# W1 loaded in two transfers with 1 KB pieces, and x transposed from every second column

## The chip, the cores and the metric

The kernel runs on one core of one Trainium2 chip. A core has five engines that run beside each other: TensorE (PE, with its weight loads shown apart as PEld), VectorE (DVE), ScalarE (ACT), GpSimd (POOL) and SyncE (SP), which here only issues transfers (DMA). Data comes from the main memory into SBUF (128 partitions); TensorE writes into PSUM, from where DVE and ACT read. The metric is the time of one execution in microseconds of device time, lower is better.

## The reference

`x` has 128 batches of 128 rows and 512 columns in float32. Each batch has a language id `itok` between 0 and 8, which picks one of ten sets of weights. The bottleneck layer, residual and normalization are

```
w1 = W1[language_ids]                      # [512, 128] of each batch
w2 = W2[language_ids]                      # [128, 512] of each batch
h = jnp.einsum('bsh,bha->bsa', hidden_states, w1) + b1[language_ids][:, None, :]
h = jax.nn.relu(h)
adapted = jnp.einsum('bsa,bah->bsh', h, w2) + b2[language_ids][:, None, :]
x = hidden_states + adapted
mean = jnp.mean(x, axis=-1, keepdims=True)
var = jnp.mean(jnp.square(x - mean), axis=-1, keepdims=True)
normed = (x - mean) * jax.lax.rsqrt(var + LN_EPS)
return normed * gamma[language_ids][:, None, :] + beta[language_ids][:, None, :]
```

and the output is the input `x` plus that result. `W1` is [10, 512, 128]: language, input column h, bottleneck column a.

## The kernel before, in words

A batch is one tile: its 128 rows lie on the 128 partitions, its 512 columns in the free dimension. `x` is loaded in groups of four batches (`load_x`, line 67, 1 MB each, with four buffers), all weights of all ten languages are loaded once at the start and stay in SBUF, and each batch picks its language's slice by a register.

**The start.** SP issues its transfers in this order (lines 85 to 108): the ids, gamma, the first two batches of x (`load_part(0, 2)`, line 83), W1 in four transfers (line 97), the other two batches of the first group, W2 in two transfers of five languages each (line 102), and the groups x_1, x_2 and x_3. ACT issues beta, b2 and b1. W1's tile `w1` is [128 partitions, 10 languages, 4 chunks, 128]. Transfer k brings chunk k: partition p gets row 128k + p of each language's W1, so a piece that is contiguous on both sides is one row of 128 values, 512 B. x and W2 come in pieces of 2 KB.

While these flow, TensorE runs some idle matmuls (`spin`, line 418), transposes the first batches, and spreads the rows of beta, gamma and b2 over all partitions (`spread`, line 155), which DVE and ACT copy out (lines 158 and 160). Then follow the down projections of batches 0 to 3, then up(0), up(1), up(2).

**One batch.** `stage_w1` (line 186): ACT copies the language's [128, 4, 128] slice of `w1` into `w1s`. `transpose_x` (line 191): TensorE turns the four chunks of 128 columns of x, one transpose each, into the PSUM tile pxT; here the chunk of x is the operand that is loaded as weights (the LDWEIGHTS records of line 191), and the identity is streamed through. `copy_xT` (line 195): ACT copies pxT to SBUF as xT. `down` (line 214): for each chunk k, w1s chunk k as weights, xT chunk k streamed, all four accumulated; as fp32, each is two passes in the profile. `relu` (line 222) on ACT. `up` (line 231), two passes of 512 columns; for the first four batches and one in four after that, a small bf16 matmul (line 230) adds b2, otherwise POOL does it (`add_b2`, line 201). POOL also prepares x + beta (`add_beta`, line 208). DVE adds the residual (line 237), centers and scales by gamma (line 281) and finishes (line 290); ACT makes the sum of squares (line 249).

**The order.** It is written out by hand: `keep` ties each instruction behind the one before it on its engine, queues included. In the steady loop the order on TensorE is transposes of batch i, down of batch i - 1, up of batch i - 2. pxT has a single buffer, so the transposes of a batch wait until ACT has copied the batch before out; py has five buffers. The chunks only have to agree between `w1` and the transposes: chunk k of xT must hold the columns of x that chunk k of `w1` holds as rows.

Of the kernel before, what the change touches and what calls it, by code (L numbers as in the profile page):

```python
# [16 lines left out]
P = 128  # L17
# [6 lines left out]
def cond_resid_kernel(ctx: ExitStack, tc: tile.TileContext, x, itok, W1, b1, W2, b2, gamma, beta, out):  # L24
# [8 lines left out]
    nc = tc.nc  # L33
    B, S, H = x.shape
    L, _, A = W1.shape
    KC = H // P
# [6 lines left out]
    def keep(ins):  # L43

        engine = ins.ins.engine
        if engine in last:
            tc.add_manual_dep(ins.ins, last[engine], behind, reason="kept order")
        last[engine] = ins.ins.name
        return ins
# [20 lines left out]
    def xb(b):  # L70
        return xs[b // G][:, b % G, :]
# [5 lines left out]
    w1 = const.tile([P, L, KC, A], FP, name="w1")  # L77
# [14 lines left out]
    warm = const.tile([P, 1], FP, name="warm")  # L92
    nc.vector.memset(warm, 1.0)
    keep(nc.scalar.activation(warm, warm, AF.Sqrt))
    for k in range(KC):
        keep(
            nc.sync.dma_start(out=w1[:, :, k, :], in_=W1[:, k * P : (k + 1) * P, :].rearrange("l p a -> p l a"))
        )
    load_part(2, G)
    for l in range(0, L, 5):  # L100
        keep(
            nc.sync.dma_start(
                out=w2[:, l * H : (l + 5) * H].rearrange("p (l h) -> p l h", l=5),
                in_=W2[l : l + 5].rearrange("l a h -> a l h"),
# [5 lines left out]
    ident = const.tile([P, P], FP, name="ident")  # L110
# [52 lines left out]
    phs, pxs, sums = {}, {}, {}  # L163
# [24 lines left out]
    def transpose_x(b):  # L188
        pxs[b] = p_x.tile([P, KC, P], FP, tag="xT", name=f"pxT_{b}")
        for k in range(KC):  # L190
            keep(nc.tensor.transpose(pxs[b][:, k, :], xb(b)[:, k * P : (k + 1) * P], ident))  # L191

    def copy_xT(b):
        xT[b] = tp.tile([P, KC, P], FP, tag="xT", name=f"xT_{b}")
# [228 lines left out]

    spin(12, H)
    transpose_x(0)
    transpose_b1()
    copy_xT(0)
    for r in range(22):
        spread(r, nc.scalar if r % 3 == 2 else nc.vector)
        if r == 5:  # L430
            transpose_x(1)
            copy_xT(1)
        elif r > 5:
            spin(1, H // 2)
# [3 lines left out]
    for b in range(4):  # L438
        down(b)
        if b < 2:  # L440
            transpose_x(b + 2)
        relu(b)
        if b < 2:
            copy_xT(b + 2)
        for r in range(22 + 3 * b, min(25 + 3 * b, R)):
            spread(r, nc.scalar if r % 3 == 2 else nc.vector)
        stage_w1(b + 2)
# [3 lines left out]
    for i in range(3, B + U):  # L451
        if i < B and i % G == 0 and i // G + 3 < NG:
            load_x(i // G + 3)
        b = i - U - 1
# [20 lines left out]
        p = g - 1  # L475
# [79 lines left out]
```

## Time and profile before

| | |
|---|---|
| median of three runs | 321.16 us (320.8 to 321.39) |
| the profiled execution: its time, its span | 321.39 us, 318.8 us |
| granted TensorE clock in it | 0.987 |
| PE, PEld busy | 305.1 us (96%), 226.0 us (71%) |
| DVE, ACT, POOL busy | 300.7 (94%), 285.5 (90%), 280.6 us (88%) |
| moved by DMA | 72.88 MB, 40,986 packets |
| transposes, L191: MATMUL, LDWEIGHTS | 512 of 273 ns, 512 of 141 ns |

The profile shows one execution; times in it count from the span's start. In a line of the order of time come the start, the length, the engine, the line of the kernel, the operation and its tiles; brackets tell how long the engine was idle just before, and what ended that. Neighbouring instructions of one kind are merged (x4). The records of matmuls overlap, since one drains while the next streams, so the work of TensorE is read from start to start. In a table of stretches each row gives the stretch, then the busy time and number of instructions of each engine, the granted clock, the share of the DMA engines and what they moved in GB/s.

### The profile page before, as it was taken

Reading aid. Unit: us, or ns where it says so; the run is one execution under the profiler, and the core shown is the slowest. Engines: PE = TensorE matmul, PEld = TensorE weight load, DVE = VectorE, ACT = ScalarE, POOL = GpSimd, SP = SyncE. Lnnn points to the kernel's source line nnn. Section 1 sums busy time; section 2 is a strip of 40 time slices with the busy share of each in tenths; the row PEclk is TensorE's granted clock in tenths of the full one; section 3 lists DMA queues with packets and bytes.
Section 4 is the critical chain, followed back from the end, with each engine's and each line's share of the span. In section 5 each row is a group of like instructions: output and inputs, shape, how many; then the busy total and the mean of one; then the engine's idle time right before and its main releaser. Section 6 shows DMA issues by size and latency. Waiting matters only on the chain. (4 is left out here: it accounts for less than half of the span.)

```text
span 318.8 us, 7184 instructions
## 1 busy us (share of the span) xinstructions
PE 305.1 (96%) x1889; PEld 226.0 (71%) x1889; DVE 300.7 (94%) x1000; ACT 285.5 (90%) x721; POOL 280.6 (88%) x234
## 2 busy tenths in 40 slices
PE   8998999999999999999999999999999999999960
PEld 3475777777777777777777777777777777777730
DVE  5946999999999999999999999999999999999995
ACT  2686989999999999999999999999999999999972
POOL 1306999999999999999999999999999999999873
PEclk9999999999999999999999999999999999999995
DMA  7997577577766666678666676678766666633324
GB/s 204 317 386 288 198 262 254 214 264 263 221 231 212 223 246 232 228 264 263 247 215 213 217 244 231 223 265 264 245 210 215 224 241 228 226 135 133 129 112 156
DMA packets 40986, 72.88 MB, mean 229 GB/s; under 512 B 1737, under 2 KB 6868, under 8 KB 40946
## 3 DMA queue, kind: packets, MB, share of 16 engines
q1 hardware_dynamic: 40886, 72.38, 66.4%
q8 instruction: 15, 0.25, 0.3%
q14 instruction: 25, 0.20, 0.2%
q10 hardware_dynamic: 60, 0.05, 0.1%
HBM read 38.86 MB, written 33.55 MB: 227 GB/s over the span
## 5 line engine op out<-in xcount | busy, mean ns | idle before, releaser
L208 POOL TENSOR_TENSOR o<-x,beta_b 128x512 f32<-128x512 f32 x128 | 162.0, 1278 | 10.6 <-DVE beta_b L160 10.6
L201 POOL TENSOR_TENSOR r<-x,b_b 128x512 f32<-128x512 f32 x93 | 118.8, 1277 | 20.0 <-DMA x<-in_x_dram 12.1
L214 PE MATMUL ph<-xT,w1s 128*128 128x128 f32 x1024 | 135.7, 275 | 0.3 <-ACT w1s L186 0.2
L231 PE MATMUL py<-w,hT 128*128 x256 | 130.9, 593 | 0.2 <-DVE o L290 0.2
L214 PEld LDWEIGHTS ph<-xT,w1s 128*128 128x128 f32 x1024 | 124.6, 192 | 2.6 <-ACT hT L222 1.3
L191 PEld LDWEIGHTS pxT<-ident,x 128*128 128x128 f32 x512 | 63.9, 141 | 67.1 <-issue 43.4
L281 DVE SCALAR_TENSOR_TENSOR py<-py,nmean,gamma_b 128x512 f32<-128x512 f32 x126 | 94.7, 752 | 0.3 <-issue 0.3
L290 DVE SCALAR_TENSOR_TENSOR o<-py,rstd,o 128x512 f32<-128x512 f32 x122 | 90.4, 741 | 1.4 <-DVE nmean L242 0.5
L249 ACT ACTIVATE sq<-py,nmean 128x512 f32<-128x512 f32 x124 | 85.3, 688 | 4.5 <-DVE nmean L242 2.9
L195 ACT COPY xT<-pxT 128x512 f32<-128x512 f32 x128 | 73.8, 577 | 12.1 <-PE pxT L191 10.1
L186 ACT COPY w1s<-w 128x512 f32 x128 | 79.5, 622 | 0.2 <-DVE gamma_b L160 0.2
L191 PE MATMUL pxT<-ident,x 128*128 128x128 f32 x512 | 77.0, 273 | 0.9 <-ACT xT L195 0.7
L237 DVE SCALAR_TENSOR_TENSOR py<-py,r 128x512 f32<-128x512 f32 x93 | 64.7, 695 | 2.5 <-POOL r L201 0.6
L222 ACT ACTIVATE hT<-ph,b1T 128x128 f32<-128x128 f32 x128 | 47.6, 372 | 1.1 <-PE ph L214 1.0
L231 PEld LDWEIGHTS py<-w,hT 128*128 128x128 f32 x256 | 41.6, 192 | 2.9 <-issue 0.9
L237 DVE SCALAR_TENSOR_TENSOR py<-py,x 128x512 f32<-128x512 f32 x35 | 24.2, 692 | 3.7 <-PE py L231 3.7
L249 ACT ACTIVATION_READ_ACCUMULATOR sq<-py,nmean 128x1 f32 x124 | 25.2, 203 | 0.0
L255 ACT ACTIVATE sd<-ssq,eps 128x2 f32<-128x2 f32 x62 | 18.3, 296 | 2.1
L242 DVE TENSOR_SCALAR nmean<-sum 128x1 f32<-128x1 f32 x128 | 18.7, 146 | 0.2
L230 PE MATMUL py<-parts,pick 96*128 96x512 bf16 x35 | 13.3, 381 | 0.0
L237 DVE DVE_READ_ACCUMULATOR py<-py,r 128x1 f32 x93 | 13.1, 141 | 0.0
L270 DVE TENSOR_TENSOR stat<-stat,y 128x2 f32<-128x2 f32 x62 | 12.8, 206 | 0.0
(54 smaller groups left out, 117.7 us busy)
## 6 DMA issues: line engine op xcount, KB each, us to landing
x<-in_x_dram SPq DMA_DIRECT2D x31, 1024.0 KB, 6.1
out_dram<-o SPq DMA_DIRECT2D x61, 512.0 KB, 3.5
w<-in_L_cond_W_dram SPq DMA_DIRECT2D x4, 640.0 KB, 6.6
w<-in_L_cond_W_dram SPq DMA_DIRECT2D x2, 1280.0 KB, 11.5
out_dram<-o SPq DMA_DIRECT2D x6, 256.0 KB, 2.2
x<-in_x_dram SPq DMA_DIRECT2D x2, 512.0 KB, 3.9
rows<-in_L_cond_beta_dram ACTq DMA_DIRECT2D x1, 20.0 KB
rows<-in_L_cond_gamma_dram SPq DMA_DIRECT2D x1, 20.0 KB
```

Source lines behind the costliest of these rows:

```text
L186: keep(nc.scalar.copy(w1s[b].rearrange("p k a -> p (k a)"), src))
L191: keep(nc.tensor.transpose(pxs[b][:, k, :], xb(b)[:, k * P : (k + 1) * P], ident))
L195: keep(nc.scalar.copy(xT[b], pxs.pop(b)))
L201: keep(nc.gpsimd.tensor_tensor(rs[b], xb(b), b2_b[:, bass.ds(v * H, H)], ALU.add))
L208: keep(nc.gpsimd.tensor_tensor(os[g][:, j, :], xb(b), beta_b[:, bass.ds(v * H, H)], ALU.add))
L214: nc.tensor.matmul(phs[b], lhsT=w1s[b][:, k, :], rhs=xT[b][:, k, :], start=(k == 0), stop=(k == KC - 1))
L222: keep(nc.scalar.activation(hT[b], phs.pop(b), AF.Relu, bias=b1T[:, bass.ds(lid(b, ET.Activation), 1)]))
L231: keep(nc.tensor.matmul(ys[b], lhsT=hT[b], rhs=w2[:, bass.ds(v * H, H)], start=not m, stop=True))
L237: keep(nc.vector.scalar_tensor_tensor(ys[b], ys[b], 1.0, r, ALU.mult, ALU.add, accum_out=s))
L249: keep(nc.scalar.activation(sq, ys[b], AF.Square, bias=nmeans[b], accum_out=ssqs[g][:, j : j + 1]))
L281: nc.vector.scalar_tensor_tensor(ys[b], ys[b], nmeans.pop(b), gamma_b[:, bass.ds(v * H, H)], ALU.add, ALU.mult)
L290: nc.vector.scalar_tensor_tensor(o, ys.pop(b), rstds[g][:, j : j + 1], o, ALU.mult, ALU.add)
```

## The change

W1 comes in two transfers. Transfer m brings the 256 rows 256m to 256m + 255 of each language, and partition p gets the two neighbouring rows 256m + 2p and 256m + 2p + 1, as chunks 2m and 2m + 1 of `w1`. A piece contiguous on both sides is two rows, 1 KB. Chunk 2m + j of `w1` so holds the rows 256m + 2p + j, and the transposes read the same columns of x: for chunk 2m + j those from 256m + j on, every second one, 128 of them. Everything else is as it was.

```
-    for k in range(KC):
+
+    for m in range(KC // 2):
         keep(
-            nc.sync.dma_start(out=w1[:, :, k, :], in_=W1[:, k * P : (k + 1) * P, :].rearrange("l p a -> p l a"))
+            nc.sync.dma_start(
+                out=w1[:, :, 2 * m : 2 * m + 2, :].rearrange("p l j a -> p l (j a)"),
+                in_=W1[:, 2 * m * P : 2 * (m + 1) * P, :].rearrange("l (p j) a -> p l (j a)", j=2),
+            )
         )
     load_part(2, G)
...
     def transpose_x(b):
         pxs[b] = p_x.tile([P, KC, P], FP, tag="xT", name=f"pxT_{b}")
         for k in range(KC):
-            keep(nc.tensor.transpose(pxs[b][:, k, :], xb(b)[:, k * P : (k + 1) * P], ident))
+            cols = xb(b).rearrange("s (m p j) -> s m j p", m=KC // 2, j=2)[:, k // 2, k % 2, :]
+            keep(nc.tensor.transpose(pxs[b][:, k, :], cols, ident))
```

## Prediction

> **What bounds the kernel now.** I read the stretches of the span first, then the groups by line, then the order of time in one steady stretch and in the start. From 100 to 300 us TensorE has no free time, and its clock is granted in full.
>
> ```profile
> core 0: us, PE busy (x) PEld busy (x) DVE busy (x) ACT busy (x) POOL busy (x), PEclk, DMA share, GB/s
> 8.00:10.00 2.00, 2.00 (x14) 1.30 (x13) 2.00 (x5) 1.66 (x3) 0.00 (x0) 1.00 1.20 290
> ...
> 16.00:18.00 2.00, 1.77 (x14) 1.52 (x14) 0.62 (x2) 1.23 (x3) 0.00 (x0) 1.00 1.05 387
> ...
> 100.00:200.00 100.00, 100.00 (x635) 75.87 (x634) 99.03 (x335) 96.15 (x247) 97.03 (x79) 1.00 0.69 237
> ```
>
> A busy PE is not yet PE at its peak, so I check it by the starts of its matmuls (columns: start, length, engine, line; lengths overlap, starts don't).
>
> ```profile
> 152.30 0.60 PE L191 MATMUL pxT<-ident,x 128*128 128x128 f32 x4
> 152.74 1.06 PE L214 MATMUL ph<-xT,w1s 128*128 128x128 f32 x8
> 153.63 1.02 PE L231 MATMUL py<-w,hT 128*128 x2
> 154.49 0.60 PE L191 MATMUL pxT<-ident,x 128*128 128x128 f32 x4
> ```
>
> From start to start: 0.44 us for 4 transposes (110 ns each), 0.89 for 8 down matmuls (111 each), 0.86 for two passes of up (430 each), 2.19 in all. One batch in four adds the b2 matmul: transposes start at 149.89, 152.30, 154.49, 156.68 and 158.87, so four batches take 8.98 us, 2.245 each. The pitches leave no gap. DVE, dense too at 99%, starts L237 of two batches at 154.86 and 157.03, 2.17 us apart: it follows closely. So whatever lengthens or shortens TensorE's order by a nanosecond per batch is seen 128 times, and whatever only moves a transfer counts just where TensorE waits for it.
>
> **The weight loads of the transposes.** In the transposes x is the operand that LDWEIGHTS loads and ident the one that streams; so the new step of two falls on LDWEIGHTS.
>
> ```profile
> 152.31 0.36 PEld L191 LDWEIGHTS pxT<-ident,x 128*128 128x128 f32 x3 [0.29 <-issue]
> 152.63 0.97 PEld L214 LDWEIGHTS ph<-xT,w1s 128*128 128x128 f32 x8
> 153.52 0.30 PEld L231 LDWEIGHTS py<-w,hT 128*128 128x128 f32 x2
> 154.06 0.14 PEld L191 LDWEIGHTS pxT<-ident,x 128*128 128x128 f32 x1 [0.24 <-ACT w1s L186]
> ```
>
> A batch's first load (154.06 to 154.20) runs beside the second pass of up, and has 0.29 us to spare before the transposes start at 154.49. The other three sit one behind the other with a pitch of (0.36 - 0.14) / 2 = 110 ns, the same as that of the matmuls that they feed. They have no cover at all.
>
> **The change, part by part.**
>
> *W1's transfers.* Four DMA issues of 1,280 pieces of 512 B become two of 1,280 pieces of 1 KB; the bytes stay (4 x 640 KB = 2.62 MB). The rows above price the pieces: 290 GB/s while W1's 512 B pieces flow (8 to 10 us), 387 while 2 KB pieces flow (16 to 18). W1 at 290 takes 9.04 us. No row has 1 KB pieces; the bounds are these two rates, 9.04 and 6.77 us, so W1 saves between 0 and 2.3 us. Between them I take a fixed part and a part per byte: over 16 engines a 512 B piece takes 28.2 ns and a 2 KB piece 84.7, so 1 KB takes 28.2 + 56.5/3 = 47 ns, 349 GB/s, 7.5 us: **W1 and all that is queued behind it on SP's queue lands 1.5 us earlier**. Against this stands the Trainium skill, "DMA: Bandwidth & Descriptors", section Specifications: 512 B is given there as the smallest transfer that reaches line rate, by which W1 would save nothing and the forecast would be no change; the trace differs, 290 against 387 GB/s.
>
> *Who waits for them.* SP issues, in order, x_0's first half, W1, x_0's second half, W2, x_1 to x_3. stage_w1(0) starts on ACT at 15.72 behind the row copies, 0.24 us after ACT's last; W1's pieces have given way to those of 2 KB by 14 us (the stretch from 14 to 16 moves 388 GB/s), so it isn't what held it. The down, transpose and row matmuls run without a DMA wait to 26.2. The first wait for a transfer is x_1's:
>
> ```profile
> 25.34 1.02 PE L231 MATMUL py<-w,hT 128*128 x2
> 26.59 0.63 PE L191 MATMUL pxT<-ident,x 128*128 128x128 f32 x4 [0.22 <-DMA x<-in_x_dram]
> 27.89 0.66 PE L191 MATMUL pxT<-ident,x 128*128 128x128 f32 x4 [0.68 <-ACT xT L195]
> ...
> 26.61 1.26 POOL L201 TENSOR_TENSOR r<-x,b_b 128x512 f32<-128x512 f32 x1 [12.13 <-DMA x<-in_x_dram]
> ```
>
> Two passes of up from 25.34 leave TensorE free at 25.34 + 0.86 = 26.20; the transposes of batch 4 start at 26.59. x_1 costs 0.39 us, and both TensorE and POOL (26.61) start as it lands. Landing 0.39 us earlier is enough; a W1 at 303 GB/s (2.62 MB in 8.65 us) would do it. What is late next is TensorE itself: up(2) ahead of these transposes, then copy_xT(4) on ACT, which the wait at 27.89 shows, and which moves with them. From 28.4 on TensorE is full, so the 0.39 is kept to the end. **-0.39 us** (bounds 0 and -0.39). POOL starts its r_4 earlier too; that is worth nothing, since DVE reads r_4 at 33.25, over 5 us after it was ready. x_2 and x_3 land earlier than they did, and TensorE never waited for them. Two DMA issues fewer on SP cost and gain nothing: nobody waits for SP in the start but for the data.
>
> *The step of two.* 512 loads of 128 columns read every second element over 1 KB in place of 512 B. No row has such a read. The nearest are the contiguous loads, 110 ns apart, and pick's broadcast loads of one element (step zero, 98 ns mean, bf16), which show no price for a pattern. Nothing is skipped in instructions or bytes used, so no gain; the lower end is 0. The upper end: the load takes as long as two contiguous loads of the span it covers, +110 ns, uncovered for three of four: 0.33 us x 128 = +42 us. I take **0**, as the row for the same number of columns is the nearest. The Trainium skill, "SBUF — State Buffer", section Door 1, says that full speed needs at least two accesses in each 16-byte line. A step of two over fp32 has exactly two, so the page makes it free, at the very edge; a step of four would not be. No run here shows it.
>
> *PSUM, copies, down.* pxT, xT, w1s keep their shapes; the copies and down matmuls read the same amounts in the same order. 0.
>
> **The sum.** The profiled execution took 321.39 us, span 318.8 and 2.6 around it: 321.39 - 0.39 = 321.0. That execution is the slowest of three; their median is 321.16, and the same step from it gives **320.8 us**.
>
> **The rivals.**
>
> *A. The strided load is slower (the other side).* Place: the three uncovered loads of each batch. Price: each ns adds 3 x 128 = 0.384 us. One ns eats the gain; from 2.7 ns (1.03 / 0.384) the kernel is slower by over 0.2%. A doubled load gives 321.0 + 42 = 363 us; 8 ns give 324. For it: the two pitches are equal, TensorE has no slack, 512 loads. Against it: nothing in the rows shows a price of a pattern. A small price 0.08, a large one 0.18.
>
> *B. The pieces of 1 KB flow no faster (the change doesn't do what it says for the queue).* x_1 lands as before: 321.2. For it: the 290 GB/s could be set by something other than the piece. Against: 2 KB pieces from the same memory on the same queue ran at 387 right behind. 0.07.
>
> *C. More is gained than x_1's wait.* With x_1 early, TensorE and ACT meet in another rhythm between 26 and 28.4, where TensorE is idle 0.39 and then 0.86 us (27.03 to 27.89). If all went: 319.9. Against: the second pause is copy_xT(4), 0.59 us, with pxT in a single buffer, which the change leaves. 0.07.
>
> **How the numbers follow.** The forecast has 0.60, its own range 320.3 to 321.4 by the scatter of the three runs (320.8 to 321.39) around the shift. What a measurement of this kernel can tell from no change is about 0.2%, 0.64 us. Forecast and B lie within it; of the forecast I give 0.10 to a measured time over 0.64 us below, so faster is 0.07 + 0.10 = 0.17. Slower is A, 0.26, and a little scatter: 0.27. Same is the rest, 0.56. The range goes from 320.1 (part of C) to 324.2 (the small price of A) and leaves out the large price.
>
> **What would show it.** Right: the rate between 6 and 12 us at some 350 GB/s with half the packets; the transposes of batch 4 at 26.2 with no DMA wait; L191's LDWEIGHTS at a mean of 141 ns, a pitch of 110, and four batches in 8.98 us. Wrong: a longer mean or pitch of L191's LDWEIGHTS, matmuls of L191 apart by more than 110 ns, and PEld busier than 76% between 100 and 200 us, which would make it rival A; 290 GB/s in place of 350, rival B.

## The result, and the profile after

The changed kernel takes 323.88 us (median of 22 runs, 322.96 to 324.99) against 320.95 us before (22 runs, 320.03 to 322.48): ratio 1.0091, 95% interval 1.0080 to 1.0102. It is 0.9% slower. The forecast was 320.8 us, a little faster: the direction is the wrong one, and the time lies in the stated range only because the range took in the small price of rival A.

Between 100 and 300 us TensorE is as dense as it was. The group rows of the transposes, line 196 in the changed kernel (busy us, then mean ns of one), point to where the time came from: the weight loads have a mean of 202 ns in place of 141, their matmuls 281 in place of 273, and the down matmuls stay at 275.

```profile
L219 PE MATMUL ph<-xT,w1s 128*128 128x128 f32 x1024 | 135.5, 275 | 0.2
L196 PEld LDWEIGHTS pxT<-ident,x 128*128 128x128 f32 x512 | 80.7, 202 | 59.8 <-issue 36.8
L196 PE MATMUL pxT<-ident,x 128*128 128x128 f32 x512 | 81.1, 281 | 0.7 <-ACT xT L200 0.7
```

A mean of overlapping records isn't a price yet. The order of time gives it, one batch, matmuls and then weight loads (start, length, engine, line):

```profile
153.33 0.63 PE L196 MATMUL pxT<-ident,x 128*128 128x128 f32 x4
153.80 1.06 PE L219 MATMUL ph<-xT,w1s 128*128 128x128 f32 x8
154.69 1.02 PE L236 MATMUL py<-w,hT 128*128 x2
155.55 0.63 PE L196 MATMUL pxT<-ident,x 128*128 128x128 f32 x4
```

```profile
152.91 0.20 PEld L196 LDWEIGHTS pxT<-ident,x 128*128 128x128 f32 x1 [0.24 <-ACT w1s L190]
153.33 0.44 PEld L196 LDWEIGHTS pxT<-ident,x 128*128 128x128 f32 x3 [0.23 <-issue]
153.68 0.98 PEld L219 LDWEIGHTS ph<-xT,w1s 128*128 128x128 f32 x8
```

From the first transpose to the first down matmul it is 0.47 us, 0.44 before; the rest of the batch is unchanged (0.89 and 0.86). Read one by one, the starts of these matmuls are 109, 117, 120 and 120 ns apart where they were 109 four times: 8 + 11 + 11 = **30 ns a batch**. The first strided load, beside a pass of up, costs nothing; the other three do. Four batches take 9.10 us (transposes at 150.89 and 159.99) in place of 8.98. Over 128 batches 30 ns are 3.84 us.

The transfers did what they were to do. W1's pieces flow at some 350 GB/s (stretches, last column):

```profile
8.00:10.00 2.00, 2.00 (x14) 1.30 (x12) 2.00 (x4) 1.58 (x3) 0.00 (x0) 1.00 1.10 348
10.00:12.00 2.00, 2.00 (x13) 1.11 (x12) 2.00 (x4) 1.25 (x3) 0.00 (x0) 1.00 1.11 352
...
14.00:16.00 2.00, 1.71 (x10) 0.84 (x9) 2.00 (x4) 1.05 (x3) 0.77 (x1) 1.00 1.05 388
```

and the transposes of batch 4, and POOL's first r, no longer follow x_1:

```profile
25.64 1.02 PE L236 MATMUL py<-w,hT 128*128 x2
26.50 0.63 PE L196 MATMUL pxT<-ident,x 128*128 128x128 f32 x4
```

```profile
23.74 1.27 POOL L206 TENSOR_TENSOR r<-x,b_b 128x512 f32<-128x512 f32 x1 [8.97 <-DMA x<-in_x_dram]
```

Batch 4 starts without a wait, but at 26.50, only 0.09 us earlier than the 26.59 of before: up(2) ends 0.30 us later. The first row matmuls start at 7.42 us, 7.14 before, since in this execution the four transposes of batch 0 ran 213 ns apart until 6.9 us; before, the third interval was 110 ns.

From there to the last matmul (26.51 to 310.60, before 26.59 to 307.62) it is 3.06 us more. That is 124 batches of 30 ns, 3.7, less 0.6 us that a second effect gave back: before, TensorE paused for 0.3 us at 48.6 and again at 67 us, after it didn't.

That second effect starts at DVE. Before the change DVE sat idle for 0.63 us until 42.77, and for 0.55 until 61.02. After such a gap ACT has to wait for DVE's `nmean`, its copies are late, and TensorE waits for pxT to be copied out. The rows of the kernel before, of DVE, ACT, and PEld near 48 and 66 us:

```profile
42.77 0.70 DVE L237 SCALAR_TENSOR_TENSOR py<-py,r 128x512 f32<-128x512 f32 x1 [0.63 <-POOL r L201]
```

```profile
44.23 0.69 ACT L249 ACTIVATE sq<-py,nmean 128x512 f32<-128x512 f32 x1 [0.41 <-DVE nmean L242]
```

```profile
48.17 0.51 PEld L191 LDWEIGHTS pxT<-ident,x 128*128 128x128 f32 x4 [0.52 <-ACT xT L195]
...
66.42 0.53 PEld L191 LDWEIGHTS pxT<-ident,x 128*128 128x128 f32 x4 [0.50 <-ACT xT L195]
```

The bracket of the first row names POOL's r, but POOL had long been done: the r that DVE reads at 42.77 is r_8, which POOL wrote from 35.22 to 36.50.

```profile
35.22 1.28 POOL L201 TENSOR_TENSOR r<-x,b_b 128x512 f32<-128x512 f32 x1
```

What ended just before 42.77 is DVE's own load of the next four language ids into registers (`lid`, line 168 before, 172 after), from 41.41 to 42.61. Such instructions aren't counted as busy, so the time looks idle. The rows of that load, before and after (duration in ns, start in us):

```profile
L168 DVEq TENSOR_LOAD <-lang x1: 1201/1201/1201, 41.4 to 41.4; - x1
```

```profile
L172 DVEq TENSOR_LOAD <-lang x1: 626/626/626, 41.4 to 41.4; - x1
```

In all 14 profiles, each of the 18 gaps of DVE over 0.2 us between 38 and 303 us is as long as the load in front of it less 0.57 us; after the short load here the gap is 0.05. Why the load takes 1.20 us at one time and 0.63 at another isn't shown.

### The profile page after: what moved, and what is told of

Its sections match the earlier page's. It is cut to its first block, busy times and chain, and to the rows that moved or that the text cites. A ratio compares the mean times of both kernels' runs of the same rounds, so it can differ in the third digit from the quotient of the medians.

```text
span 322.2 us, 7180 instructions
## 1 busy us (share of the span) xinstructions
PE 308.5 (96%) x1889; PEld 236.8 (74%) x1889; DVE 304.7 (95%) x1000; ACT 284.1 (88%) x721; POOL 281.1 (87%) x234
## 5 line engine op out<-in xcount | busy, mean ns | idle before, releaser
L219 PEld LDWEIGHTS ph<-xT,w1s 128*128 128x128 f32 x1024 | 125.9, 193 | 1.9 <-ACT hT L227 0.8
L196 PEld LDWEIGHTS pxT<-ident,x 128*128 128x128 f32 x512 | 80.7, 202 | 59.8 <-issue 36.8
L196 PE MATMUL pxT<-ident,x 128*128 128x128 f32 x512 | 81.1, 281 | 0.7 <-ACT xT L200 0.7
```

The source lines that it names most:

```text
L196: keep(nc.tensor.transpose(pxs[b][:, k, :], cols, ident))
L219: nc.tensor.matmul(phs[b], lhsT=w1s[b][:, k, :], rhs=xT[b][:, k, :], start=(k == 0), stop=(k == KC - 1))
```

## The experiments

My theory after the result: the strided loads cost 30 ns a batch, where they have no cover; the transfers alone are a gain. The first rival: the transfers' new landing times upset the rhythm, and the loads are innocent. The second: every strided load costs alike, covered or not. Each kernel of an experiment was run 4 to 12 times, beside the kernel before.

The measured time is the span and what lies around it, which is not the same in all runs: mostly 1.8 us, in others up to 3.2. So the table gives the median span too, and I compare small differences by spans.

| kernel | us | ratio to before, 95% | median span (before) |
|---|---|---|---|
| changed kernel | 323.88 | 1.0091 (1.0080 to 1.0102) | 322.0 (profiled: 318.8) |
| e1 pieces only | 319.79 | 0.9961 (0.9948 to 0.9975) | 318.0 (318.8) |
| e2 step only | 323.92 | 1.0096 (1.0080 to 1.0111) | 322.05 (318.8) |
| e3 first pair | 322.06 | 1.0035 (1.0021 to 1.0048) | 319.8 (318.8) |
| e4 last pair | 322.73 | 1.0056 (1.0042 to 1.0070) | 321.0 (318.8) |
| e5 step four | 324.19 | 1.0099 (1.0077 to 1.0120) | 321.9 (318.8) |
| e6 step three | 322.3 | 1.0045 (1.0030 to 1.0060) | 320.4 (318.8) |
| e7 x_1 in halves | 319.56 | 0.9965 (0.9951 to 0.9979) | 317.7 (318.8) |
| e8 step, halves | 323.23 | 1.0082 (1.0061 to 1.0104) | 321.4 (318.8) |
| e9 changed, 10 idle | 323.31 | 1.0085 (1.0062 to 1.0108) | 321.35 (318.9) |
| e10 halves, 10 idle | 320.32 | 0.9984 (0.9968 to 1.0000) | 317.75 (318.9) |
| e11 before, 10 idle | 321.52 | 1.0019 (1.0007 to 1.0032) | 318.95 (318.9) |
| e12 changed, halves | 322.89 | 1.0060 (1.0041 to 1.0080) | 321.1 (318.9) |

**e1, the transfers alone.** The changed kernel with the old line of the transposes:

```
-            cols = xb(b).rearrange("s (m p j) -> s m j p", m=KC // 2, j=2)[:, k // 2, k % 2, :]
-            keep(nc.tensor.transpose(pxs[b][:, k, :], cols, ident))
+            keep(nc.tensor.transpose(pxs[b][:, k, :], xb(b)[:, k * P : (k + 1) * P], ident))
```

> W1 in two transfers of 1 KB pieces, the transposes read contiguous columns as before; it so multiplies rows of W1 with the wrong columns of x, with the same instructions and times. Theory (the strided weight loads cost 30 ns a batch, the transfers save what x_1's wait was worth): 0.1 to 0.4 us under the kernel before, some 320.6 to 320.9 us beside 320.95, W1's stretch at 350 GB/s, the transposes of batch 4 with no DMA wait, intervals of the transposes 109 ns. Rival (the transfers' new landing times upset the rhythm and the strided loads are innocent): 323.9.

319.79 us, faster than I had expected. Batch 4 starts at 26.08 with no wait for a transfer (0.51 earlier than before), r_4 starts at 24.88 in place of 26.61, and of the two pauses of 0.6 us together 0.13 is left. The rival falls, and the transfers are worth more than TensorE's own wait. (The kernel's result isn't the reference's; its time is what counts here.)

**e2, the step alone.** W1 in four transfers of 512 B pieces, each with every second row:

```
+        m, j = divmod(k, 2)
+            rows_k = W1[:, 2 * m * P : 2 * (m + 1) * P, :].rearrange("l (p j) a -> j p l a", j=2)[j]
+        keep(nc.sync.dma_start(out=w1[:, :, k, :], in_=rows_k))
```

> The step of two alone: W1 in four transfers of 512 B pieces as before, each with every second row, so that the result is the reference's. Theory: the changed kernel's time plus what its transfers saved, 323.9 to 324.4 us; intervals between matmuls at the transposes 109, 117, 120, 120 ns in place of four of 109, a period of 2.275 us a batch in place of 2.248. Rival (the transfers did it): 321.

323.92 us; the four intervals are 109, 117, 120 and 120 ns, the period 2.275 us. The step carries the loss by itself.

**e3 and e4, one pair of chunks strided, the other contiguous.** The step of two only where `k // 2` is 0 (e3) or 1 (e4), W1's rows to match:

```
+            cols = xb(b)[:, k * P : (k + 1) * P]
+            if k // 2 in (0,):            # e4: (1,)
+                cols = xb(b).rearrange("s (m p j) -> s m j p", m=KC // 2, j=2)[:, k // 2, k % 2, :]
```

> The step of two for chunks 0 and 1 alone, contiguous chunks 2 and 3, W1 in four transfers of 512 B pieces. Theory (only a strided load that stands beside a matmul of 109 ns costs; the first load of a batch stands beside a pass of up of 430 ns and is free): one uncovered load, 8 to 11 ns a batch, 1.0 to 1.4 us, 321.9 to 322.4. Rival (each strided load costs alike, 7.5 ns): 15 ns a batch, 1.9 us, 322.8, the same as with the last pair.

> The step of two for chunks 2 and 3 alone, contiguous chunks 0 and 1, W1 in four transfers of 512 B pieces. Theory (two uncovered strided loads): 8 + 11 = 19 to 22 ns a batch, 2.3 to 2.8 us, 323.2 to 323.7. Rival (each strided load costs alike): 15 ns a batch, 1.9 us, 322.8, the same as with the first pair.

The same number of strided loads, and the spans differ: 1.0 us over before with the first pair, 2.2 with the last. The order of time, first e3, then e4, shows it: 0.44 us from the first transpose to down with the first pair (one interval of 117), 0.46 with the last (117, then 122 on average).

```profile
152.57 0.61 PE L197 MATMUL pxT<-ident,x 128*128 128x128 f32 x4
153.01 1.06 PE L220 MATMUL ph<-xT,w1s 128*128 128x128 f32 x8
```

```profile
153.13 0.62 PE L197 MATMUL pxT<-ident,x 128*128 128x128 f32 x4
153.59 0.61 PE L220 MATMUL ph<-xT,w1s 128*128 128x128 f32 x4
```

So cover decides, and the rival with alike prices falls. e4's time came out 0.5 us under what I had expected, though its intervals are a little longer; by the profiles, batch 4 starts 0.23 us earlier in e4 than in the kernel before.

**e5 and e6, other steps.** e5 takes W1 in one transfer of 2 KB pieces and every fourth column; e6 changes only which columns are read:

```
+            cols = xb(b).rearrange("s (p j) -> s j p", j=KC)[:, k, :]                          # e5
...
+            lo = P * (k // 3)                                                                  # e6
+            cols = xb(b)[:, lo : lo + 3 * P].rearrange("s (p j) -> s j p", j=3)[:, k % 3, :]
```

> A step of four: W1 in one transfer of 2 KB pieces (four neighbouring rows to a partition), chunk j of x every fourth column from j on. Theory (a strided load occupies the read for longer, and the first of a batch is covered) leaves two sizes open. If the price doubles when each access of 4 bytes falls into a 16-byte line of its own: loads of some 213 to 240 ns, three uncovered, 0.33 to 0.40 us a batch, 362 to 371 us. If it rises evenly with the step (120 ns at two, from at most 109 at one): some 140 ns, 30 ns each, 0.09 us a batch, 333 us. Rival (a strided pattern costs one fixed price whatever its step): 120 ns, 323 to 324 us.

> A step of three in the transposes alone, the four chunks taken from columns 0, 1, 2 and 128 on; W1 stays as before, so rows of W1 meet the wrong columns of x, with the same instructions. If the price goes by the number of 16-byte lines touched (32 for 128 contiguous values, 64 at a step of two, 96 at three, 128 at four): between the steps of two and four. If it goes by a price per access that has its line to itself: likewise between, nearer to four. Rival (a fixed price): as at a step of two, 324 us.

Step four costs what step two costs, to the nanosecond: intervals 109, 117, 120, 120, weight loads of 202 ns. Step three is cheaper, on average 109, 112, 116 and 115 (single ones lie between 109 and 121), weight loads of 195. The rows of e5, then e6:

```profile
L193 PEld LDWEIGHTS pxT<-ident,x 128*128 128x128 f32 x512 | 80.5, 202 | 59.4 <-issue 36.5 <-ACT w1s L187 20.9 <-ACT xT L197 2.0
```

```profile
L193 PEld LDWEIGHTS pxT<-ident,x 128*128 128x128 f32 x512 | 78.1, 195 | 60.5 <-issue 36.3 <-ACT w1s L186 19.9 <-ACT xT L197 3.3
```

The prices that grow with the step, or with the number of 16-byte lines, both fall. The fixed price fits steps two and four, but not three. What sets the price stays open.

**e7, x_1 in two halves, nothing else.** If an earlier x_1 was the gain of e1, it can be had with contiguous columns:

```
+    x_1 = xp.tile([P, G, H], FP, tag="x", name="x_1")
+    xs[1] = x_1
+    for lo in (0, 2):
+        keep(
+            nc.sync.dma_start(
+                out=x_1[:, lo : lo + 2, :], in_=x[G + lo : G + lo + 2].rearrange("b s h -> s b h")
+            )
+        )
-    for g in range(1, 4):
+    for g in range(2, 4):
         load_x(g)
```

> The kernel before, with x_1 in two transfers of two batches each, W1 in four and contiguous transposes. Theory (the gain of the transfers alone was x_1's landing: TensorE waited for it 0.39 us, and POOL, which is busy without a pause from r_4 at 26.6 to some 70 us, falls behind so far that DVE and then TensorE wait another 0.6 us between 45 and 68 us): its first half lands 1.35 us earlier (0.52 MB at 387 GB/s), 0.7 to 1.1 us faster, 319.9 to 320.3. Rival (what I had predicted: only TensorE's wait counts): 0.4 us, 320.6. Rival (the 1 KB pieces gained by something else): no change.

319.56 us, the fastest of all, with W1 as it was, and 0.3 us under the range that I had expected. r_4 starts 1.72 us earlier, and TensorE has none of the pauses between 28 and 303 us:

```profile
24.89 1.26 POOL L209 TENSOR_TENSOR r<-x,b_b 128x512 f32<-128x512 f32 x1 [10.34 <-DMA x<-in_x_dram]
```

```profile
25.39 1.02 PE L239 MATMUL py<-w,hT 128*128 x2
26.25 0.60 PE L199 MATMUL pxT<-ident,x 128*128 128x128 f32 x4
```

The time bears out that an earlier x_1 is worth more than TensorE's wait, and the two rivals fall. It doesn't bear out my theory of POOL. DVE still has a gap at 42 us, 0.26 us long in place of 0.63, and its register load there took 0.84 us in place of 1.20. In none of the 14 profiles did DVE read an r, or an x + beta, less than 5.3 us after POOL had written it. What holds over all profiles is the pairing: in the seven where r_4 starts before 25 us, TensorE's pauses come to between 0 and 0.13 us, in the seven where it starts later, to between 0.2 and 0.7. How x_1's landing acts on the register load isn't shown.

**e8, the step of two and x_1 in halves** (e2 and e7 together).

> The step of two with W1 in four transfers of 512 B pieces, and x_1 in two halves. If an earlier x_1 is worth the same beside strided loads as beside contiguous ones: 1.0 us under the step alone (323.92), 322.9. If it is worth next to nothing there, as the changed kernel (323.88) beside the step alone suggests: 323.6 to 323.9. No pause of TensorE between 45 and 70 us in either case.

323.23 us, 0.7 under the step alone by time and by span, nearer to the first expectation; no pause of TensorE. So an earlier x_1 helps beside strided loads too. Then why is the changed kernel no faster than e2, the step alone? By the two profiles it is 0.53 us faster from batch 4 to the last matmul, and loses that by a start that is 0.34 us later and by 0.39 us more behind the last matmul.

**e9 to e12, the start.** `spin(10, H)` for `spin(12, H)` in the changed kernel (e9), in e7 (e10) and in the kernel before (e11); the halves of e7 in the changed kernel (e12).

> The changed kernel with 10 idle matmuls ahead of the first transposes in place of 12. In its profile the clock stayed low until 6.9 us, the first transposes began at 6.27 and ended late, and the row matmuls began at 7.42, against 6.4 to 7.2 in seven other profiles; by this theory the start took back what an earlier x_1 gave, and a shorter start gives it again: 0.4 to 0.8 us under the changed kernel, 323.1 to 323.5. Rival (an earlier x_1 is worth nothing beside strided loads, whatever the start): 323.9.

> Contiguous transposes, W1 in four transfers, x_1 in two halves, 10 idle matmuls. With x_1's first half landed at 24.8 us, TensorE's own order sets when batch 4 begins, so a shorter start counts: 0.2 to 0.6 us under the halves alone (319.56), 319.0 to 319.4. Rival (the picks on DVE at 6.1 to 6.9 us, not TensorE, set when the rows begin): 319.5.

> The kernel before with 10 idle matmuls. The theory that x_1's landing (26.0 to 26.5 us) sets when batch 4 begins says that a shorter start is waited away: 320.8 to 321.0, as the kernel before. Rival (the start's own length counts here too): 320.3 to 320.5.

> The changed kernel with x_1 in two halves. Its x_1 already lands at 23.6 us, before TensorE or POOL can use it, so a still earlier first half gives nothing: 323.9. If the transfers' landing still costs something in the changed kernel, as e8 (323.23, without 1 KB pieces, but in halves) might say: 323.2.

e9 is 0.6 us under the changed kernel: batch 4 starts at 25.43 in place of 26.50. By their times e10 and e11 missed what was expected of them, by their spans they fit. e11 keeps the span of the kernel before (318.95 and 318.9), as it should if x_1's landing sets the start there; its time is 0.8 us longer, nearly all of it around the span. e10 has the span of e7 (317.75 and 317.7), so a shorter start gains nothing there: in its profile the rows wait for pick on DVE (0.53 us, to 7.12), as the rival said; its time is 0.8 us longer for the same reason as e11's. e12 missed: 322.89, 0.9 us of span under the changed kernel, though x_1 had been early enough already. Its profile has the row matmuls at 7.06 in place of 7.42 and batch 4 at 26.13 in place of 26.50; from there to the last matmul the two take the same, 284.08 and 284.09 us. In that profile another 0.39 us of gain lie behind the last matmul. e9 differs from the changed kernel in the start alone, but for 0.1 us. What makes the start late can be read in part: in each profile the matmuls of the start double their pace at some moment (the idle ones from 430 ns apart to some 215), at 4.5 us in e2, not before 6.9 in the changed kernel. The profile's clock column shows 1.00 on both sides of it. What sets that moment, and whether it is late in most runs of the changed kernel, stays open with one profile of each.

## Why the prediction was wrong, point by point

**The bound** was right: TensorE has no slack between 100 and 300 us, and a few ns in each batch showed in full.

**W1's transfers** were right in rate: 349 GB/s was worked out, 348 to 352 measured. That all behind W1 lands 1.5 us earlier came out too: of the 16 landings that the trace records for x_1, 15 came by 25.23 us before and by 23.69 in e1. r_4 waits for the last one, and that is uneven: it let r_4 start 1.7 us earlier in e1, 2.9 in the changed kernel.

**What waits for them** was right in its first term, too small in all. TensorE's wait of 0.39 us went as said. "From 28.4 on TensorE is full, so the 0.39 is kept to the end" failed: the kernel before has two more pauses of TensorE, 0.6 us in all, behind long register loads of DVE, and they are gone or small wherever x_1 lands earlier. e1 and e7, where both terms go, are 0.8 and 1.1 us of span faster. "POOL starts its r_4 earlier too; that is worth nothing" isn't refuted: in no profile did DVE come within 5.3 us of POOL's r. Whether POOL's earlier start acts in another way isn't shown. Rival C, more gained than x_1's wait, was right by its number (319.9), but by luck: its place was the pause at 27 to 28 us, which stayed.

**The step of two** is the term that failed and turned the sign. "I take 0, as the row for the same number of columns is the nearest": the row was one of contiguous reads and said nothing of strided ones. In place of 0 stand 30 ns a batch, 3.84 us over 128, as e2 shows without the new transfers and e1 without the step. The working beside it was right and held the answer: three loads without cover, one with, 0.384 us for each ns; rival A with a small price of 8 ns gave 324, and the mean of three is 10. It had 0.08. I had reckoned with a load that is free or takes twice as long, and put little on a load that is a tenth longer than the matmul that covers it.

**The rule that I weighed**, two accesses in each 16-byte line (the Trainium skill, "SBUF — State Buffer", section Door 1), made the step of two free and a step of four not. The runs contradict it on both counts: step two costs 8 to 11 ns a load without cover, step four the same, step three less.

**The sum.** Predicted -0.39; measured in the profiles, up to the last matmul: 3.7 us for the loads behind batch 4, -0.6 for the two pauses, -0.08 at batch 4 (x_1's 0.39 less a start 0.30 later), +3.0 in all. The spans differ by 3.4, as 0.4 us more lie behind the last matmul; by medians of time it is +2.93.

## What to carry to other kernels

Before the access pattern of an operand in an inner loop is changed to save on a transfer that runs once, multiply what one ns of it costs: here 384 loads without cover, 0.38 us for each ns, against a transfer whose whole worth was about 1 us. Look for the transfer that is really waited for; cutting x_1 in two gave the gain of larger W1 pieces for nothing (0.35% faster than before, the best kernel here). Before a wait is laid to the engine that the profile names, ask when that engine's tile was ready: here r had been ready for 6 us, and the wait was for an instruction that isn't counted as busy.

## What the runs showed of the hardware that was not expected

- A weight load of 128 fp32 columns at a step of two or four sustains one in 120 ns, at a step of three one in 112 to 116 on average, contiguous one in 109 or less (these rows are set by the matmul beside it). Nothing is seen of it where the matmul beside it takes 430 ns, nor in batch 0 of the changed kernel, where the strided transposes stood 213 ns apart, as contiguous ones did in e7. What inside the load takes longer isn't shown; the steps rule out a price that grows with the step.
- Pieces of 512 B, 1 KB and 2 KB on the same queue flowed at 290, 350 and 387 GB/s.
- DVE's load of four language ids into registers takes some 0.62 us in most places, but up to 1.47 us near 41, 50 and 60 us. DVE's next instruction starts 0.16 us after it, whatever its length, wherever the load takes 0.6 us or more.
- In the kernel before, 15 of the 16 landings of x_1 had come by 25.2 us, the last came at 26.45; a packet of 16 KB of the instruction queue, 1.09 us long, starts in the trace at 22.5 us. In the changed kernel all 16 had come by 23.6, and the late one is the last of x_2. That the packet delays the landing isn't shown.
- The time around the span is 1.8 us in most runs, up to 3.2 in others, and for e10 2.4 or more in all of twelve runs.
